# A four-layer graph kernel: layer norm's factors by blocks, and the first d ahead of the packings

## The chip, the cores and the metric

The kernel runs on one core of a Trainium2 chip. The time is the device time of one execution in microseconds (us); for the kernel before, the median of three runs is 541.25 us (540.78 to 541.6). A profiled execution is slower than these and is told apart from them.

A core has five queues of instructions that matter here, each worked off in its own order: PE (matrix products; PEld loads their weights), DVE (vector operations), ACT (activation functions and copies), POOL (here gathers by index, and a few fills) and SP (plain DMA transfers). Between them stand waits: an instruction starts when what it reads has been written and what it overwrites has been read.

## The reference

There are 2,708 nodes with 128 features, `x`, and an adjacency matrix `adj` of 2,708 by 2,708, of which about 0.3% are not zero; the entries of a row are all equal. Four layers follow one another, each of them with a layer norm and a ReLU ahead and added to its input:

```python
h = jnp.maximum(_layernorm(x, axis=-1), 0.0)
x = x + _L0_gnn_ref(h, adj, ...)      # hyperbolic maps around  adj @ log_map_zero(h)
h = jnp.maximum(_layernorm(x, axis=-1), 0.0)
x = x + _L1_gnn_ref(h, adj, ...)
# inside L1, for each pair i, j with an edge:
s = node_feats @ msg_w[:, :D].T
d = node_feats @ msg_w[:, D:].T
messages = gelu(s[:, None, :] + d[None, :, :] + msg_b)
aggregated = jnp.einsum('ijd,ij->id', messages, adj)
```

Layers 2 and 3 are products with `adj` again. The change lies in layer 0 and in what prepares layer 1.

## The kernel before

**Tiles.** The nodes lie in 22 tiles of 128 (the last has 20 nodes). Tiles go in six blocks, `groups[0]` to `groups[5]`: five of four tiles and one of two. Blocks 0 to 2 are the first half (12 tiles), blocks 3 to 5 are called `late`. `adj` transposed is read once, block by block, and kept as a mask of zeros and ones in one byte each (`read_block`, lines 1014 to 1055).

**Layer 0, product.** For each block the PE multiplies the mask with the node features, which are split into three bf16 parts: `add_product` (line 1359) does 22 tiles by 3 parts, 66 matmuls, into one accumulator `acc`; `end_product` (line 1375) squares and copies it and sums the squares (`nsq`). `neighbours` (line 1408) then makes the hyperbolic factors, `update` (line 1449) adds the result to `x` and takes the layer norm's statistics (`bn_stats`), and `normal_form` (line 944) makes scale and bias of the norm (`rstd`, `nb`) from them: 15 small DVE instructions, each needing the last.

**Edges.** In the same stretch the edges are found. `words_in` (line 1073) packs a block's mask into words: 22 matmuls `pk` on PE, a copy `wt` on ACT, transposes `wp` on PE, and a copy back. The last block is narrower than its tiles, so that POOL fills the rest of `wt` with zeros first (line 1082). `find_words`, `find_columns` and `lay_out` on DVE make lists of neighbours from the words; `val` is gathered by POOL for each tile (line 1160), and `po` is a small matmul in `lay_out` (line 1256).

**Preparing layer 1.** `make_d` (line 1473) takes a block: ACT makes h from x with `rstd` and `nb` (line 961), PE transposes it (`hTpm`, line 971), it is copied (`hT`, line 972), PE multiplies it with the message weights (`d`, line 983), ACT copies the result (line 1480) and SP writes it to tables in HBM (line 1483): to `d_hbm`, which holds all nodes, and to `d_early`, two small tables with the first two and the first three blocks. The two first places of each tile's list of neighbours, the early places, are filled from `d_early` while layer 0 still runs (`gather_early`, line 1577, on POOL, one gather for one tile and place); the other places are gathered from `d_hbm` in layer 1 (line 1793), after its last write.

**What sets the order.** The function's text gives an order, but a planner lays out each engine's instructions by its own costs, and `queue_behind(i)` says that what follows is not placed ahead of instruction i. The built program's order on each engine is fixed.

**Layer 1 to 3.** Layer 1 goes tile by tile: POOL gathers, DVE adds, ACT makes the gelu, PE sums (lines 1802 to 1880), and products for layer 2 are put between. Layers 2 and 3 follow.

Of the kernel before, what the change touches and what calls it, by code (L numbers as in the profile page):

```python
# [51 lines left out]
BLOCK = 4  # L52
SLOTS = 24
HEAD = 6
EARLY = 2
# [501 lines left out]
def sparse_stack(  # L557
# [21 lines left out]
    nc = tc.nc  # L579
    N = x_in.shape[0]  # L580
    T = -(-N // P)
    NP = T * P
    full = N // P
# [27 lines left out]
    hT = state.tile([P, NP], F32, name="hT")  # L611
# [98 lines left out]
    early_c = state.tile([P, T, EARLY], U32, name="early_c")  # L710
# [55 lines left out]
    def queue_behind(ins):  # L766
        return ExitStack() if ins is None else tc.issue_after(ins.ins)
# [56 lines left out]
    with ExitStack() as st:  # L824
# [52 lines left out]
        def node(name):  # L877
            if name not in names:
                names[name] = wide.tile([P, T], F32, name=f"n_{name}")
            return names[name]  # L880
# [4 lines left out]
        def norm(sq, sl, name):  # L885

            a, r, n, q = (node(c + name)[:, sl] for c in "arnq")
            nc.vector.tensor_scalar_max(a, sq, NORM_EPS * NORM_EPS)
            rsqrt(a, r, q)
            nc.vector.tensor_mul(n, a, r)  # L890
            return a, r, n
# [52 lines left out]
        def normal_form(sl):  # L944

            t, a, r, nb, q = (node(name)[:, sl] for name in ("tn", "an", "rstd", "nb", "qn"))
            nc.vector.tensor_sub(t, bst[:, sl, 1], bst[:, sl, 4])
            nc.vector.tensor_mul(t, t, t)
            nc.vector.tensor_add(a, bst[:, sl, 2], bst[:, sl, 5])
            nc.vector.scalar_tensor_tensor(a, t, float(D // 4), a, op0=ALU.mult, op1=ALU.add)  # L950
            nc.vector.tensor_scalar(a, a, 1.0 / D, LN_EPS, op0=ALU.mult, op1=ALU.add)
            rsqrt(a, r, q)
            nc.vector.tensor_add(t, bst[:, sl, 1], bst[:, sl, 4])
            return nc.vector.scalar_tensor_tensor(nb, t, -0.5, r, op0=ALU.mult, op1=ALU.mult)
# [21 lines left out]
        def tiles_times(sl, aT, w, name, mirrored=False):  # L976

            n = sl.stop - sl.start
            ps = ps_one.tile([P, BANK], F32, tag="one", name=name)
            wide_by = w.shape[-1]  # L980
            for k in range(n):
                t = sl.stop - 1 - k if mirrored else sl.start + k
                latest["times"] = nc.tensor.matmul(  # L983
                    ps[:, k * wide_by : (k + 1) * wide_by],
                    aT[:, t * P : (t + 1) * P],
                    w,
                    start=True,
                    stop=True,
                )
            return ps[:, : n * wide_by].rearrange("p (n d) -> p n d", d=wide_by)  # L990
# [62 lines left out]
        def read_block(b):  # L1053
            for g in pieces:
                read_piece(b, g)
# [17 lines left out]
        def words_in(b, after=None):  # L1073

            t0, t1 = blocks[b]
            n = t1 - t0
            sl = cols(t0, t1)
            w = sl.stop - sl.start
            pk = pack(b, after)
            wt = words_p.tile([P, BANK], F32, tag="wt", name=f"wt{b}")  # L1080
            if w < n * P:
                nc.gpsimd.memset(wt[:, w : n * P], 0.0)
            nc.scalar.copy(wt[:, :w], pk[:, :w])
            ps = ps_one.tile([P, BANK], F32, tag="one", name=f"wp{b}")
            for k in range(n):
                nc.tensor.transpose(ps[:, k * P : (k + 1) * P], wt[:, k * P : (k + 1) * P], ident)
            key = wt.bitcast(I32)
            nc.scalar.copy(key[:, : n * P], ps[:, : n * P])
            return key
# [78 lines left out]
        def each(c, n):  # L1168
            return c.unsqueeze(1).to_broadcast([P, n, EARLY])
# [189 lines left out]
        def add_product(b, acc, ts, after=None):  # L1359

            sl = cols(*blocks[b])
            w = sl.stop - sl.start
            for t in ts:
                for k in range(3):
                    with queue_behind(after):
                        last = nc.tensor.matmul(  # L1366
                            acc[:, :w],
                            parts[:, t, k, :],
                            mask[:, t, sl],
                            start=(t == 0 and k == 0),  # L1370
                            stop=(t == T - 1 and k == 2),
                        )
            return last
# [72 lines left out]
            nc.vector.tensor_add(dot[:, sl], dot[:, sl], node("dot0")[:, sl])  # L1446
            return last

        def update(bs):

            sl = slice(blocks[bs[0]][0], blocks[bs[-1]][1])
            f, ca, cb = node("f")[:, sl], node("ca"), node("cb")
            _, r, n = norm(node("sq")[:, sl], sl, "u")
            log_factor(node("nsq")[:, sl], f, sl)
            moebius(f, r, n, node("dot")[:, sl], y2_layer, ca[:, sl], cb[:, sl], sl)
            for b in bs:
                g = groups[b]
                n = g.stop - g.start
                for t in range(g.start, g.stop):
                    nc.vector.scalar_tensor_tensor(  # L1460
                        x[:, t, :], own[:, t, :], ca[:, t : t + 1], x[:, t, :], op0=ALU.mult,
                        op1=ALU.add,
                    )
                for t in range(g.start, g.stop):
                    nc.vector.scalar_tensor_tensor(
                        x[:, t, :], layer_b, cb[:, t : t + 1], x[:, t, :], op0=ALU.mult,
                        op1=ALU.add,
                    )
                for t in range(g.start, g.stop):
                    nc.vector.bn_stats(bst[:, t, :], x[:, t, :])  # L1470
            return normal_form(sl)

        def make_d(bs, copy, after=None, relu_after=None):

            for b in bs:
                g = groups[b]
                normal_tiles(g, f"m{b}", copy, after, relu_after)
                ps = tiles_times(g, hT, msg_w[:, 1, :], f"d{b}", mirrored=True)
                d = v[:, g, :]
                nc.scalar.copy(d, ps)  # L1480
                for table, end in ((d_early[0], reach[0]), (d_early[1], reach[1]), (d_hbm, T)):
                    if g.stop <= end:
                        nc.sync.dma_start(
                            out=table[(end - g.stop) * P : (end - g.start) * P, :].rearrange(
                                "(t p) d -> p t d", p=P
                            ),
                            in_=d,
                        )
# [88 lines left out]
        def gather_early(ts, ks):  # L1577
            for t in ts:
                for k in ks:
                    nc.gpsimd.indirect_dma_start(  # L1580
                        out=early_d[t // EACH][:, t % EACH, k, :],
                        out_offset=None,
                        in_=d_early[k],
                        in_offset=bass.IndirectOffsetOnAxis(ap=early_c[:, t, k : k + 1], axis=0),
                    )
# [17 lines left out]
        sums = sums_of([2])  # L1603
        product(2, sums)
        times = times_layer([2])
        formed = update([0, 1])
        read_block(4)
        acc = begin_product(3)
        last = add_product(3, acc, range(2 * BLOCK))
        read_block(5)  # L1610
        words[4] = words_in(4, last)
        last = latest["pack"]
        make_d([0], nc.scalar.copy, last)
        last = add_product(3, acc, range(2 * BLOCK, 3 * BLOCK), last)
        words[5] = words_in(5, last)
        last = latest["pack"]
        lay_out(halves[0])
        with queue_behind(scaled):
# [10 lines left out]
                is_place, place_k, 0.0, is_place, op0=ALU.is_ge, op1=ALU.mult  # L1629
            )  # L1630
        done = neighbours([2], sums, formed, times)
        make_d([1], nc.scalar.copy, last, latest["th"])
        find_words(3, words[3])
        find_columns(groups[3])
        for k in range(-(-T // EACH)):
# [7 lines left out]
        end_product(3, acc, sums)  # L1643
        acc = begin_product(4)
        last = add_product(4, acc, range(2 * BLOCK))
        formed = update([2])
        find_words(4, words[4], done)
        find_words(5, words[5], done)
        make_d([2], nc.scalar.copy, last)
        add_product(4, acc, range(2 * BLOCK, T), last)  # L1650
        end_product(4, acc, sums)
        product(5, sums)
        find_columns(slice(groups[3].stop, T))
        gather_early(range(first_half), [1])
        lay_out(halves[1])
        for b in (0, 1):
            mark_edges(b, formed)
        last = neighbours(late, sums)

        with queue_behind(last):  # L1660
            nc.vector.tensor_add(early_c[:, halves[1], :], late_c, each(none_c, T - first_half))
        gather_early(range(first_half, full), range(EARLY))
        formed = update(late)
        make_d(late, nc.vector.tensor_copy)
        for b in (2, *late):
            mark_edges(b, formed)
# [457 lines left out]
```

## Time and profile before

| | |
|---|---|
| median of three runs | 541.25 us |
| profiled execution | 634.93 us |
| its span, from first to last instruction | 633.2 us |
| mean granted clock of PE in it | 0.841 of full |
| busy in it: PE, DVE, ACT, POOL | 439.5, 425.7, 243.1, 234.4 us |
| layer 0 and preparing layer 1 (to the first gather from `d_hbm`) | 0 to 238.5 us |
| gathers of layer 1 | 238.5 to 477.8 us |
| rest | 477.8 to 633.2 us |

A group of the profile is read so: line and engine, operation, tile written and tiles read (without buffer numbers), how often; then the busy time in us and the mean duration in ns; then the idle time of the engine just ahead of it, and what ended most of it. In a timeline, the first number is the start in us from the span's beginning, the second the length, and the bracket the idle time ahead and what ended it. "issue" means that nothing is shown that the engine waited for, "remote" and "another core or an unknown queue" that what released it is not known.

### The profile page before, as it was taken

The page shows a single profiled execution, that of the slowest core. Times are in us where ns is not written, and L with a number is a line of the kernel's source. Part 1 is how long each engine was busy: PE and PEld are TensorE (multiplying, and loading weights), DVE is VectorE, ACT ScalarE, POOL GpSimd, SP SyncE. Part 2 cuts the span into 40 slices and gives each one's busy share as a digit, 9 for nine tenths or more (in the row PEclk, how much of TensorE's full clock was granted, in tenths as well). Part 3 has the DMA queues.
Part 4 walks back from the last instruction along what each step waited for, and adds up shares of the span by engine and source line. Part 5 has one row for each costly group of instructions (what it writes and reads, how often), then busy time and mean ns, then how long its engine had stood idle before and what let it go on. Part 6 is the DMA issues. An engine that isn't in the chain of part 4 may idle for free.

```text
span 633.2 us, 8305 instructions
## 1 busy us (share of the span) xinstructions
PE 439.5 (69%) x2504; PEld 278.4 (44%) x2504; DVE 425.7 (67%) x1805; ACT 243.1 (38%) x576; POOL 234.4 (37%) x269
## 2 busy tenths in 40 slices
PE   2955999997185061335756658737849898989995
PEld 1641445453144051234625436525636544545553
DVE  7959869988314975533758557646736669998752
ACT  3787668872012133112534423423435544510000
POOL 8600132015551747755754655655741000000000
PEclk9986999999595556656778977977979999989999
DMA  8884698613020121211315345344310024079311
GB/s 278 261 300 146 227 332 284 188 53 85 15 68 16 46 71 41 51 41 44 89 43 191 104 130 162 95 125 152 103 38 10 1 89 175 2 285 391 128 37 57
DMA packets 40420, 78.41 MB, mean 124 GB/s; under 512 B 5818, under 2 KB 19702, under 8 KB 38810
## 3 DMA queue, kind: packets, MB, share of 16 engines
q1 hardware_dynamic: 31326, 63.67, 29.2%
q0 software_dynamic: 7296, 13.40, 8.4%
q10 hardware_dynamic: 1744, 0.72, 0.4%
q8 instruction: 22, 0.36, 0.2%
q14 instruction: 32, 0.26, 0.1%
HBM read 73.63 MB, written 4.14 MB: 123 GB/s over the span
## 4 chain that ended last, share of the span: by engine, by line
DVE 34%; PE 29%; another core or an unknown queue 11%; issue 11%; ACT 8%; DMA 5%; POOL 2%; ACTq 0%; DVEq 0%; POOLq 0%
PE three L1732 8%; PE two L1732 4%; PE msg L1855 4%; DMA a<-in_adj_t_dram 2%; PE msg L1857 2%; DMA layer_w<-in_L_gnn_layer_dram 2%; DVE eq L1748 2%; PE own L801 2%; PE d L983 1%; POOL g L1793 1%; PE u L1516 1%; ACT mask L1034 1%; PE acc L1366 1%; PE neigh L1771 1%
## 5 line engine op out<-in xcount | busy, mean ns | idle before, releaser
L1732 PEld LDWEIGHTS <-parts 128*128 128x128 bf16 x792 | 76.1, 101 | 85.6 <-issue 8.0
L1793 POOL DMA_INDIRECT g<-d_hbm,head_c x84 | 83.2, 991 | 75.6 <-issue 39.0
L1732 PE MATMUL two<-mask,parts 128*128 128x512 fp8e4 (+1 forms) x396 | 85.0, 370 | 5.8 <-ACT parts L1717 5.5
L1366 PE MATMUL acc<-mask,parts 128*128 128x512 fp8e4 (+1 forms) x396 | 84.0, 366 | 6.2 <-issue 5.8
L1732 PE MATMUL three<-mask,parts 128*128 128x512 fp8e4 (+1 forms) x396 | 80.5, 359 | 0.6 <-ACT parts L1717 0.5
L1793 POOL DMA_INDIRECT gt<-d_hbm,tail_c x65 | 62.6, 963 | 27.5 <-issue 18.3
L1366 PEld LDWEIGHTS <-parts 128*128 128x128 bf16 x396 | 38.0, 102 | 53.6 <-issue 9.3
L1580 POOL DMA_INDIRECT early<-d_early,early_c x42 | 42.2, 1005 | 49.7 <-issue 21.4
L1855 PE MATMUL msg<-ident,early 128*128 128x128 f32 x84 | 19.1, 364 | 56.7 <-DVE gt L1844 27.2
L1160 POOL DMA_INDIRECT val<-in_adj_dram,ai x22 | 21.0, 957 | 78.1 <-DVE left L1148 64.2
L1034 ACT ACTIVATE mask<-a 128x2048 fp8e4<-128x2048 uint32 (+3 forms) x27 | 38.2, 1431 | 9.2 <-DMA a<-in_adj_t_dram 8.7
L1855 PEld LDWEIGHTS msg<-ident,early 128*128 128x128 f32 x84 | 14.9, 248 | 60.4 <-issue 43.3
L1748 DVE TENSOR_SCALAR_CACHE_REDUCE eq<-row,val 128x2708 fp8e4<-128x2708 f32 (+1 forms) x13 | 39.4, 3030 | 1.1 <-DMA row<-in_adj_dram 1.0
L1064 PE MATMUL pk<-mask,shifts 128*128 128x512 fp8e4 (+1 forms) x132 | 30.9, 374 | 12.5 <-ACT mask L1034 12.5
L1844 DVE TENSOR_TENSOR gt<-gt,msg 128x384 f32<-128x384 f32 (+1 forms) x22 | 12.0, 544 | 29.9 <-remote 28.4
L1855 PE MATMUL msg<-ident,g 128*128 128x128 f32 x168 | 31.5, 348 | 0.0
L1808 PE MATMUL msg<-parts,r_all 128*128 128x128 bf16 x195 | 15.0, 224 | 22.5 <-issue 18.5
L1855 PEld LDWEIGHTS msg<-ident,g 128*128 128x128 f32 x168 | 29.9, 262 | 0.5
L1831 DVE TENSOR_TENSOR rt<-col_i,tail_r 128x384 f32<-128x384 f32 (+1 forms) x22 | 12.0, 552 | 26.8 <-remote 21.7
L1748 DVE TENSOR_SCALAR_CACHE_REDUCE eq<-hT,val 128x1354 fp8e4<-128x1354 f32 x18 | 29.2, 1620 | 0.1
L1850 ACT ACTIVATE gt<-gt 128x384 f32<-128x384 f32 (+1 forms) x22 | 11.4, 517 | 37.9 <-DVE gt L1844 23.5
L1869 ACT COPY aggs<-msg 128x128 f32<-128x128 f32 x22 | 5.7, 261 | 51.4 <-remote 31.3
(408 smaller groups left out, 919.8 us busy)
## 6 DMA issues: line engine op xcount, KB each, us to landing
a<-in_adj_t_dram SPq DMA_DIRECT2D x25, 1024.0 KB
row<-in_adj_dram SPq DMA_DIRECT2D x12, 1354.0 KB
hT<-in_adj_dram SPq DMA_DIRECT2D x18, 677.0 KB
a<-in_adj_t_dram SPq DMA_DIRECT2D x5, 296.0 KB
g<-d_hbm,head_c POOLq DMA_INDIRECT x84
a<-in_adj_t_dram SPq DMA_DIRECT2D x5, 256.0 KB
d_early<-v SPq DMA_DIRECT2D x5, 256.0 KB
d_hbm<-v SPq DMA_DIRECT2D x5, 256.0 KB
```

The lines of the kernel that those rows point to most:

```text
L801: nc.tensor.matmul(ps[:, k, :, :], hT[:, (t + k) * P : (t + k + 1) * P], pair_w[:, 0::2, :], start=True, stop=True,)
L1034: nc.scalar.activation(mask[:, g : g + n, sl], bits[:, :n, :w], AF.Sign, saturate=False)
L1064: latest["pack"] = nc.tensor.matmul(pk[:, :w], shifts[:, t, :], mask[:, t, sl], start=(t == 0), stop=(t == T - 1),)
L1160: nc.gpsimd.indirect_dma_start(out=val[:, t : t + 1], out_offset=None, in_=flat, in_offset=bass.IndirectOffsetOnAxis(ap=ai[:, t : t + 1], ...
L1366: last = nc.tensor.matmul(acc[:, :w], parts[:, t, k, :], mask[:, t, sl], start=(t == 0 and k == 0), stop=(t == T - 1 and k == 2),)
L1580: nc.gpsimd.indirect_dma_start(out=early_d[t // EACH][:, t % EACH, k, :], out_offset=None, in_=d_early[k], in_offset=bass.IndirectOffsetOn ...
L1732: last = nc.tensor.matmul(accs[b][:, : sl.stop - sl.start], parts[:, t, k, :], mask[:, t, sl], start=(t == 0 and k == 0), stop=(t == T - 1 ...
L1748: last = nc.vector.tensor_scalar(eq[:n, : c1 - c0], a, val[:n, t : t + 1], None, op0=ALU.is_equal, op1=ALU.add, accum_out=same[:n, t, k : ...
L1793: nc.gpsimd.indirect_dma_start(out=g[:n, q, :], out_offset=None, in_=d_hbm, in_offset=bass.IndirectOffsetOnAxis(ap=table[:n, q : q + 1], a ...
L1808: latest["source"] = nc.tensor.matmul(ps[:, q * D : (q + 1) * D], r_all[:, t, q * P : (q + 1) * P], parts[:, t, k, :], start=(k == 0), sto ...
L1855: nc.tensor.matmul(sums, part, ident, start=(q == 0), stop=False)
L1857: done = nc.tensor.matmul(sums, gt[:, q, :], rt[:, q, :], start=(not own_places and q == 0), stop=(q == nq - 1),)
```

## The change

Four things are changed in layer 0.

- `update` takes a list `ends` of blocks after which `normal_form` is made, each time for the tiles since the last. The first call, for blocks 0 and 1, makes it after each of the two; the last, for blocks 3 to 5, after block 4 and after block 5. The call for block 2 makes one, as before.
- `make_d` of blocks 0 and 1 goes ahead of the packings of blocks 4 and 5 on PE, with tiles of product 3 between. It stood behind the packing of block 4 and of block 5.
- `make_d` of block 2 has four tiles of product 4 between its transposes and its product with the weights (`between`).
- The early places of the late tiles are gathered in another order: the late tiles' first place goes ahead of the first half's second place. For it, `early_c`, the index, is made in two pieces, one for each place, where it was one; `lay_out` of the second half stands ahead of these gathers.

```diff
-        def update(bs):
+        def update(bs, ends):
 
             sl = slice(blocks[bs[0]][0], blocks[bs[-1]][1])
             f, ca, cb = node("f")[:, sl], node("ca"), node("cb")
+            form = None
...
                 for t in range(g.start, g.stop):
                     nc.vector.bn_stats(bst[:, t, :], x[:, t, :])
-            return normal_form(sl)
-
-        def make_d(bs, copy, after=None, relu_after=None):
+                if b in ends:
+                    form = slice(form.stop if b > ends[0] else sl.start, g.stop)
+                    last = normal_form(form)
+            return last
+
+        def make_d(bs, copy, after=None, relu_after=None, between=None):
 
             for b in bs:
                 g = groups[b]
                 normal_tiles(g, f"m{b}", copy, after, relu_after)
-                ps = tiles_times(g, hT, msg_w[:, 1, :], f"d{b}", mirrored=True)
+                with queue_behind(between() if between else None):
+                    ps = tiles_times(g, hT, msg_w[:, 1, :], f"d{b}", mirrored=True)
...
-        formed = update([0, 1])
+        formed = update([0, 1], [0, 1])
         read_block(4)
         acc = begin_product(3)
-        last = add_product(3, acc, range(2 * BLOCK))
+        last = add_product(3, acc, range(6))
+        make_d([0], nc.scalar.copy, last)
+        last = add_product(3, acc, range(6, 9), last)
         read_block(5)
+        make_d([1], nc.scalar.copy, last)
+        last = add_product(3, acc, range(9, 3 * BLOCK), last)
         words[4] = words_in(4, last)
-        last = latest["pack"]
-        make_d([0], nc.scalar.copy, last)
-        last = add_product(3, acc, range(2 * BLOCK, 3 * BLOCK), last)
-        words[5] = words_in(5, last)
+        words[5] = words_in(5, latest["pack"])
         last = latest["pack"]
         lay_out(halves[0])
...
         done = neighbours([2], sums, formed, times)
-        make_d([1], nc.scalar.copy, last, latest["th"])
         find_words(3, words[3])
...
-        formed = update([2])
+        formed = update([2], [2])
         find_words(4, words[4], done)
         find_words(5, words[5], done)
-        make_d([2], nc.scalar.copy, last)
-        add_product(4, acc, range(2 * BLOCK, T), last)
+        make_d(
+            [2],
+            nc.scalar.copy,
+            last,
+            between=lambda: add_product(4, acc, range(2 * BLOCK, 3 * BLOCK), last),
+        )
+        add_product(4, acc, range(3 * BLOCK, T), last)
         end_product(4, acc, sums)
         product(5, sums)
         find_columns(slice(groups[3].stop, T))
+        lay_out(halves[1])
+        early_tail = early_c[:, halves[1], :]
+        nc.vector.tensor_add(
+            early_tail[:, :, 0:1], late_c[:, :, 0:1], each(none_c, T - first_half)[:, :, 0:1]
+        )
+        gather_early(range(first_half, full), [0])
         gather_early(range(first_half), [1])
-        lay_out(halves[1])
         for b in (0, 1):
             mark_edges(b, formed)
         last = neighbours(late, sums)
 
         with queue_behind(last):
-            nc.vector.tensor_add(early_c[:, halves[1], :], late_c, each(none_c, T - first_half))
-        gather_early(range(first_half, full), range(EARLY))
-        formed = update(late)
+            nc.vector.tensor_add(
+                early_tail[:, :, 1:], late_c[:, :, 1:], each(none_c, T - first_half)[:, :, 1:]
+            )
+        gather_early(range(first_half, full), [1])
+        formed = update(late, [late[-2], late[-1]])
         make_d(late, nc.vector.tensor_copy)
```

## The prediction

> **What bounds the kernel now.** I read the page first, then the answer by cores (one core, mean granted clock 0.841), the chain of waits, and the timeline of layer 0 from 95 us on, engine by engine.
>
> ```profile
> span 633.2 us, 8305 instructions
> DVE 34%; PE 29%; another core or an unknown queue 11%; issue 11%; ACT 8%; DMA 5%; POOL 2%; ACTq 0%; DVEq 0%; POOLq 0%
> L1793 POOL DMA_INDIRECT g<-d_hbm,head_c x84 | 83.2, 991 | 75.6 <-issue 39.0
> L1793 POOL DMA_INDIRECT gt<-d_hbm,tail_c x65 | 62.6, 963 | 27.5 <-issue 18.3
> ```
>
> The profiled execution took 634.93 us (span 633.2, 1.7 around it), the median of the runs is 541.25, 93.7 less. The second line names where I look for those: 11% of the span (71.6 us) ends on an unknown queue, waits that no semaphore of the program explains. I treat them as the profiled execution's own; everything below is a shift in us, carried over to the median.
>
> The message passing of layer 1 gathers 84 + 65 = 149 times on POOL, one each 1.25 us where POOL is not held (0.94 plus 0.30 of issue): 186 us. In the profile it takes 238.5 to 477.8, 239 us. What follows takes 155 us. In a run of 541 us, 155 behind it leaves its end near 384 and its start near 198 to 209: there POOL goes nearly back to back, so what moves the first g gather moves the end by as much.
>
> Next the first gather. In the timeline (start, length, engine, line, what; in brackets the idle time before and who ended it) of POOL:
>
> ```profile
> 130.40 0.21 POOL L1082 MEMSET wt<- 128x108 f32 x1
> 146.30 0.95 POOL L1580 DMA_INDIRECT early<-d_early,early_c  x1 [15.69 <-DMA d_early<-v]
> ...
> 229.05 0.94 POOL L1580 DMA_INDIRECT early<-d_early,early_c  x1 [0.30 <-issue]
> 238.54 1.17 POOL L1793 DMA_INDIRECT g<-d_hbm,head_c  x1 [8.55 <-DMA d_hbm<-v]
> ```
>
> So g waits for the last d_hbm write, not for the early gathers. Behind that write stand make_d and update of the late chunks, and these begin when PE has finished products 4 and 5. PE's timeline:
>
> ```profile
> 127.99 4.91 PE L1064 MATMUL pk<-mask,shifts 128*128 128x512 fp8e4 x22
> ...
> 139.58 0.44 PE L1086 MATMUL wp<-ident,wt 128*128 128x128 f32 x2
> ...
> 148.23 1.04 PE L1389 MATMUL nsq<-ones_col,hT 128*128 128x1 f32 x8
> ...
> 172.46 2.07 PE L983 MATMUL d<-pair_w,hT 128*128 128x128 f32 x8 [17.55 <-ACT hT L972]
> ```
>
> and of ACT and DVE what PE waited for, and what waited for PE; last a line of the chain of waits:
>
> ```profile
> 171.82 0.59 ACT L972 COPY hT<-hTpm 128x512 f32<-128x512 f32 x1 [20.62 <-remote]
> ...
> 198.99 0.17 DVE L1413 TENSOR_TENSOR n_nsq<-nsq,val 128x10 f32<-128x10 f32 x1 [1.08 <-PE nsq L1389]
> ```
>
> ```profile
> 235.20 2.49 DMA d_hbm<-v
> ```
>
> PE stands still nowhere from 124 to 154 us; then ACT waits 20.62 us for nothing named. Without that, PE's d goes at 154.9 and ends at 156.05 (1.15, as the one at 141.21); 38 matmuls of 512 columns by 0.216 (22 packings from 127.99 to 132.74) make 164.25, 66 of 148 columns by 0.067 (30 in 2.09) and 1.05 of nsq 169.75, and 1.9 from po to the last nsq 171.65. So n_nsq, which opens the late chunks, is at 171.7 undisturbed. From there to the landing the profile has 237.69 - 198.99 = 38.7, less 2.0 that DVE's hT copy is held at 229.72: 36.7. **d_hbm lands at 208.4.** POOL undisturbed: 12 early gathers from 146.3 to 161.5, six val to 169.0, 12 and 18 more early ones to 206.5 (208.7 if some stretch as they do in the profile, where the 18 took 24.5). The two paths lie 2 us apart, d_hbm's behind.
>
> [...]2.49 for d_hbm and 3.3 from the end of d's copy (142.97) to the first early gather. [...]2.07 for the eight d passes after 17.55 us of standing, 1.14 in the busy stretch.
>
> **The change, part by part.** I compared the order in which both kernels, built, stand on each engine.
>
> *Form by blocks, first update.* update([0, 1]) ends in two normal_forms instead of one: 15 DVE instructions more (0.08 each where others lie between, 0.20 where each waits for the last). The first stand between the 12 instructions of block 1: 121.4 + 12 x 0.26 + 15 x 0.08 puts block 0's n_nb at 125.6 (127.5 now), block 1's at 128.6, since its chain takes 3.1 us as now, only 1.2 later. So neighbours([2]) starts 1.2 later. DVE is not what the end hangs on here: 13 us of its work lie between 149.4 and PE's 171.7.
>
> *First d ahead of the packings.* PE: 12 matmuls of acc 3, transposes of block 0, d, block 1, d, then packings 4 and 5. The same matmuls, moved ahead of 6.6 us of packings. Transposes now follow ACT's relus directly: PE is there at 126.7, the third relu at 127.1, and the copy of hT comes behind one mask on ACT: 0.3 + 0.4 of standing, **0.7** (0 to 1.5). SP's six writes of the two d (two d_early and one d_hbm each, 0.36 to 0.56 of issue) move ahead too; SP's last read of block 5 was issued at 125.7, so they pass nothing. Block 1's d ends at 133.7, ACT copies it by 134.4 (four squares of neighbours first), and POOL can gather at 134.4 + 3.3 = **137.7** instead of 146.3.
>
> *What is queued behind that wait.* In the new order POOL has six early gathers in front of the memset of wt (L1082), which now stands ahead of them at 130.40. The memset fills the tail of block 5's words; PE's second wp transpose waits for POOL. Six gathers by 1.25 from 137.7: the memset ends at 145.4. PE would be at the transposes at: d 133.7, three matmuls 0.65, packing 4 4.75, packing 5 and wp 4 2.2, two matmuls 0.4: 141.6. **PE stands 3.8 us** (2.5 to 5: both times hang on the same d, so their difference is firmer than each). Queued behind it: po, all of acc 3's rest, acc 4 and 5. DVE waits for po as well, and layer-norm of block 2 with it: n_off at 146.0, the rest of update([2]) and its form (1.7 + 0.6 + 3.75 with find_words between) end at 152.6; ACT has a relu of block 2 ahead of acc 3's square, so nsq follows at 153.7 where PE is at 152.95: **0.7** more (0 to 1.5). [...]
>
> *find_words 4 and 5* move behind update([2]): DVE reaches find_columns at 157, 8 us later; its 13 us end at 171, ahead of PE's 176.9, so nothing. But ai is ready at 160 (151.65 now), and POOL's val gathers wait there from 153.
>
> *make_d([2]) with four more tiles of product between* (12 matmuls instead of 4): d_early's second table 1.7 us later, at 166; POOL wants it at 179. Nothing.
>
> *Early places.* The 42 gathers stay; 9 go ahead, on a 10-wide addition more (0.17). POOL: 12 to 153, val 160.3 to 167.8, 9 to 179, 21 to 205.3. Now 206.5: 1.2 gained on the path that does not set the start.
>
> *Form by blocks, late update.* Block 4's form no longer waits for block 5's six instructions, but shares DVE with them: n_nb at 220.9 instead of 221.54; ACT's relus 0.6 earlier. Then marks stand in front of DVE's hT copy: 223.7 for 223.96. The rest is a chain of PE, DVE and ACT as before. **0.3 gained** (0 to 1.6, the whole of block 5's instructions).
>
> Sum: 0.7 + 3.8 + 0.7 - 0.3 = **+4.9**: n_nsq of the late chunks at 176.9, d_hbm at 213.3 for 208.4, POOL free at 205.3. 541.25 + 4.9 = 546.1; in terms of the profiled execution 634.93 + 4.9 = 639.8, if its own waits stayed, which they need not.
>
> **Rivals.** *The standing is covered* (POOL comes to the memset before PE comes to wp, or PE has enough spare time after): for it, that all these times are rebuilt, not read; against it, that the gathers cannot start sooner than d's landing, and d is only 8 us of PE work ahead of wp. Then +0.7 - 0.3: 541.6. *Faster:* not d_hbm but POOL's last early gather opens the messages undisturbed. Place: POOL after 184; price: 1.2 by the count, up to 3.4 if the 18 stretch to 208.7 as in the profile, say 2.2: 539.0. It decides only if d_hbm lands today before 200.4 (205.3 less the 4.9), 8 us sooner than I rebuilt; against it speaks the 8.55 that POOL waits in the profile, for it that 93.7 us of that execution are its own and I placed them by inference. *Dearer:* the half clock, a longer standing and late ai together: +8, 549.3.
>
> **Numbers.** Forecast 0.60 (own range 543.5 to 548.5), covered 0.15, faster 0.13, dearer 0.12. Range 540.9 to 549.0: it takes in forecast, covered and the near half of dearer, and leaves out most of faster. 0.2% is 1.1 us, about what the three runs' spread (0.8) lets one tell. Faster 0.13; same 0.11, most of the covered case; slower 0.76.
>
> **What the profile will show.** Right: POOL's memset behind six early gathers, PE's second wp transpose idle for 2.5 to 5 us and ended by that memset; the first early gather 8 to 9 us sooner against PE's packings; DVE's n_off waiting for po; g again ended by d_hbm. Wrong: wp without idle time; or g following early gathers directly, with POOL never idle before it.

## The result, and the profile after

The kernel before took 541.75 us in this comparison (median of 13 runs, 538.34 to 543.89), the changed kernel 547.07 us (13 runs, 542.66 to 549.18). The ratio is 1.0095, with a 95% interval of 1.0068 to 1.0121: 5.3 us slower, where 4.9 was forecast. The profile of before that the prediction read held some 94 us of waits that no run had (634.93 us for 541.25). A second profile of the same kernel (run e1 below, span 538.1 us) has none, so that a profiled execution is not slower as such; "before" in this part means the second one. Ratios leave out slow runs, those over 1.5% above the fastest of the same kernel: in e7 these are two of 17 (543.49 and 544.41 us).

From the page of the changed kernel: the span, the chain by engine, and the two groups of gathers.

```profile
span 545.1 us, 8338 instructions
DVE 35%; PE 28%; DMA 11%; ACT 10%; issue 9%; POOL 5%; ACTq 0%; DVEq 0%; SPq 0%; POOLq 0%
L1810 POOL DMA_INDIRECT g<-d_hbm,head_c x84 | 83.4, 993 | 32.3 <-issue 20.7 <-DMA d_hbm<-v 7.0 <-ACT jx L1720 0.6
L1810 POOL DMA_INDIRECT gt<-d_hbm,tail_c x65 | 64.2, 988 | 19.8 <-issue 16.2 <-ACT parts L1736 0.6 <-ACT u L1892 0.6
```

No share of the chain ends on an unknown queue here. POOL, in the timeline of the changed kernel (start, length, engine, line, what, idle time before and who ended it):

```profile
137.49 0.94 POOL L1585 DMA_INDIRECT early<-d_early,early_c  x1 [7.14 <-DMA d_early<-v]
...
143.78 0.95 POOL L1585 DMA_INDIRECT early<-d_early,early_c  x1 [0.30 <-issue]
144.73 0.21 POOL L1082 MEMSET wt<- 128x108 f32 x1
...
205.34 1.16 POOL L1585 DMA_INDIRECT early<-d_early,early_c  x1 [0.31 <-issue]
213.51 0.95 POOL L1810 DMA_INDIRECT g<-d_hbm,head_c  x1 [7.01 <-DMA d_hbm<-v]
```

The fill stands behind six early gathers, and the first g waits 7.01 us for the last write of d_hbm. PE of the same kernel:

```profile
128.78 1.16 PE L983 MATMUL d<-pair_w,hT 128*128 128x128 f32 x8 [1.20 <-ACT hT L972]
...
141.20 0.33 PE L1086 MATMUL wp<-ident,wt 128*128 128x128 f32 x1
144.99 0.48 PE L1086 MATMUL wp<-ident,wt 128*128 128x128 f32 x1 [3.46 <-POOL wt L1082]
145.33 8.79 PE L1366 MATMUL acc<-mask,parts 128*128 128x512 fp8e4 x33
```

The second transpose stands 3.46 us for the fill, as forecast, and the 33 matmuls behind it take 8.79 us. The trace shows the clock that they had. By windows of time (from and to, length, PE's busy time, its instructions, its granted clock as a share of full, the share of DMA and GB/s):

```profile
141.00:145.00 4.00, 0.54 (x4) 1.00 0.18 49
145.00:148.00 3.00, 3.00 (x9) 0.50 0.19 49
148.00:149.00 1.00, 1.00 (x6) 0.79 0.26 66
149.00:154.00 5.00, 5.00 (x26) 1.00 0.19 52
```

From 145 to 148 us the clock is at half; a mean of 0.79 in the microsecond behind is another 0.42 us of half clock (0.21 by 0.5), 3.4 us in all. The late d's of this kernel have a granted clock of 0.50 too (198 to 206 and 206 to 210 us) and take 2.07, 2.08 and 1.19 us; block 0's d, above, takes 1.16 at a granted 1.00 (128.5 to 130 us). By these times a d is said below to run at half or at full clock. And DVE:

```profile
145.54 0.17 DVE L1257 COPY n_off<-po 128x12 f32<-128x12 f32 x1 [5.38 <-PE po L1256]
...
175.81 0.17 DVE L1413 TENSOR_TENSOR n_nsq<-nsq,val 128x10 f32<-128x10 f32 x1 [0.34 <-PE nsq L1389]
```

The start of a profile differs by up to 2.5 us between executions (block 2's `ne` product starts at 120.18 to 122.70 us, with variants of both kernels near both ends). So below, times are counted from the start of that product, which stands ahead of everything that was changed. "Copy" is the start of ACT's last copy of d (line 1480 before, 1485 in the changed kernel), "POOL free" the end of the last early gather; the last column is span less start of g.

| kernel (one profile of each) | n_nsq of the late blocks | copy | POOL free | first g | from g to the end |
|---|---|---|---|---|---|
| before (e1) | 47.97 | 82.04 | 86.05 | 86.35 | 331.6 |
| changed | 53.40 | 87.15 | 84.09 | 91.10 | 331.6 |
| e2 fill first | 48.91 | 82.40 | 80.60 | 86.21 | 331.1 |
| e3 fill last | 60.29 | 92.14 | 82.73 | 96.16 | 333.2 |
| e4 d ahead alone | 53.54 | 87.60 | 84.84 | 91.52 | 330.9 |
| e5 d back | 48.94 | 81.05 | 86.28 | 86.59 | 331.7 |
| e6 fill first, early order back | 48.67 | 82.52 | 78.80 | 86.76 | 330.9 |
| e7 fill first, unread matmuls | 48.57 | 79.36 | 79.19 | 83.53 | 330.8 |
| e8 before, unread matmuls | 47.95 | 79.68 | 86.44 | 86.75 | 332.4 |
| e9 stand filled | 51.65 | 83.51 | 82.10 | 87.59 | 332.1 |
| e10 e7 and marks behind | 48.79 | 78.99 | 78.71 | 83.66 | 335.4 |
| e11 e7 again | 48.17 | 81.09 | 78.29 | 84.46 | 331.2 |
| e12 unread matmuls throughout | 48.76 | 79.47 | 79.36 | 82.84 | 331.8 |

From g to the end, the changed kernel and the kernel before take the same 331.6 us: all 4.75 us by which the two profiles differ from that product on lie ahead of the first g.

### The profile page after: what moved, and what is told of

The parts are those of the page before. It is cut to its first block, busy times and chain, and to the rows that moved or that the text cites. A ratio compares the mean times of both kernels' runs of the same rounds, so it can differ in the third digit from the quotient of the medians.

```text
span 545.1 us, 8338 instructions
## 1 busy us (share of the span) xinstructions
PE 418.4 (77%) x2504; PEld 263.8 (48%) x2504; DVE 426.4 (78%) x1836; ACT 242.9 (45%) x576; POOL 236.4 (43%) x269
## 4 chain that ended last, share of the span: by engine, by line
DVE 35%; PE 28%; DMA 11%; ACT 10%; issue 9%; POOL 5%; ACTq 0%; DVEq 0%; SPq 0%; POOLq 0%
PE three L1749 9%; DMA a<-in_adj_t_dram 6%; PE acc L1366 5%; PE msg L1872 3%; POOL g L1810 3%; DVE eq L1765 3%; ACT mask L1034 2%; DMA g<-d_hbm,head_c 2%; PE two L1749 2%; DMA layer_w<-in_L_gnn_layer_dram 2%; ACT h L1730 1%; PE msg L1874 1%; PE d L983 1%; DVE gt L1861 1%; DVE g L1858 1%
## 5 line engine op out<-in xcount | busy, mean ns | idle before, releaser
L1749 PEld LDWEIGHTS <-parts 128*128 128x128 bf16 x792 | 74.4, 99 | 80.1 <-ACT parts L1734 4.9
L1749 PE MATMUL two<-mask,parts 128*128 128x512 fp8e4 (+1 forms) x396 | 81.8, 359 | 3.8 <-ACT parts L1734 3.5
L1366 PEld LDWEIGHTS <-parts 128*128 128x128 bf16 x396 | 37.1, 100 | 46.3 <-ACT parts L786 7.5
L1872 PE MATMUL msg<-ident,early 128*128 128x128 f32 x84 | 16.7, 329 | 30.8 <-DVE gt L1861 22.6
L1872 PEld LDWEIGHTS msg<-ident,early 128*128 128x128 f32 x84 | 13.0, 218 | 34.5 <-DVE gt L1861 12.8
L961 ACT ACTIVATE h<-x,n_nb,n_rstd 128x128 f32<-128x128 f32 x44 | 18.3, 485 | 20.7 <-DVE n_qn L778 11.5
L1872 PE MATMUL msg<-ident,g 128*128 128x128 f32 x168 | 27.2, 313 | 0.0
L1872 PEld LDWEIGHTS msg<-ident,g 128*128 128x128 f32 x168 | 25.5, 228 | 0.2
L1825 PEld LDWEIGHTS <-r_all 128*128 128x128 fp8e4 x195 | 13.1, 104 | 19.9 <-issue 14.0
L1858 DVE TENSOR_TENSOR g<-g,v 128x512 f32<-128x512 f32 x21 | 14.4, 688 | 10.3 <-DMA g<-d_hbm,head_c 9.7
L971 PE MATMUL hTpm<-ident,h 128*128 128x128 f32 x22 | 5.7, 353 | 21.0 <-ACT h L961 21.0
```

What stands on the lines that cost most here:

```text
L961: nc.scalar.activation(h[:, t, :], x[:, t, :], AF.Relu, bias=node("nb")[:, t : t + 1], scale=node("rstd")[:, t : t + 1],)
L1366: last = nc.tensor.matmul(acc[:, :w], parts[:, t, k, :], mask[:, t, sl], start=(t == 0 and k == 0), stop=(t == T - 1 and k == 2),)
L1749: last = nc.tensor.matmul(accs[b][:, : sl.stop - sl.start], parts[:, t, k, :], mask[:, t, sl], start=(t == 0 and k == 0), stop=(t == T - 1 ...
L1825: latest["source"] = nc.tensor.matmul(ps[:, q * D : (q + 1) * D], r_all[:, t, q * P : (q + 1) * P], parts[:, t, k, :], start=(k == 0), sto ...
L1858: nc.vector.tensor_add(a, a, v[:, t, :].unsqueeze(1).to_broadcast([P, a.shape[1], D]))
L1872: nc.tensor.matmul(sums, part, ident, start=(q == 0), stop=False)
```

## Experiments

**e1: the kernel before again.**

> The kernel before, unchanged, for a second profile of it: the first held some 92 us of waits of its own, and the prediction rebuilt the stretch around them. Theory (d's last write to d_hbm opens layer 1's messages): in a profile without those waits n_nsq of the late blocks stands at 171.7 us, POOL is done with the early gathers at 206.5 to 208.7, and the first g gather waits 1 to 2 us for d_hbm, at about 208.9. Rival (POOL's own early gathers open the messages): g follows the last early gather by 0.3 us, with d_hbm landed before it. Time in both cases about 541.7 us.

Measured: 539.91 us in its one run. POOL and DVE in its timeline:

```profile
205.27 0.96 POOL L1580 DMA_INDIRECT early<-d_early,early_c  x1 [0.30 <-issue]
206.53 1.08 POOL L1793 DMA_INDIRECT g<-d_hbm,head_c  x1 [0.30 <-issue]
```

```profile
168.15 0.17 DVE L1413 TENSOR_TENSOR n_nsq<-nsq,val 128x10 f32<-128x10 f32 x1 [0.95 <-DMA val<-in_adj_dram,ai]
```

The rival is right: g follows the last early gather by 0.30 us. But not by much. The chain of waits shows POOL's sequencer (POOLq) done with its waits of line 1793, that for d_hbm among them, ahead of g. First e1, then the changed kernel, where g waits for d_hbm alone:

```profile
205.73 0.04 POOLq L1793
205.78 0.76 issue
```

```profile
212.78 0.04 POOLq L1810
212.82 0.70 issue
```

In both, g follows the second of these lines directly. With the 0.70 us of the changed kernel in place of 0.76, d_hbm would have let g go in e1 at 206.47, 0.06 us sooner than it went. Two paths end within 0.1 us of each other. The DVE line shows a wait that the prediction did not have: n_nsq waits for POOL's val gathers, which stand behind twelve early gathers here, and not for PE.

**e2: the fill ahead of the early gathers.** One instruction of POOL is moved in the changed kernel.

```diff
-                nc.gpsimd.memset(wt[:, w : n * P], 0.0)
+                latest["fill"] = nc.gpsimd.memset(wt[:, w : n * P], 0.0)
...
-        gather_early(range(first_half), [0])
+        with queue_behind(latest["fill"]): gather_early(range(first_half), [0])
```

> The changed kernel with one instruction moved: POOL's fill of the last words (memset of wt) stands ahead of the early gathers, as in the kernel before; every other engine's order is untouched. Theory (the standing of PE behind that fill is the loss): PE's second wp transpose no longer stands (3.46 us in the changed kernel's profile), the 33 matmuls behind it go at 0.216 us each for 0.266 (8.79 us become 7.1), n_nsq of the late blocks is at 170.7 for 175.8 us, and the time falls by 3.5 to 5.1 us from the changed kernel's 547.07, to 542.0 to 543.6. Rival (the loss lies in the earlier d, the forms by blocks or the gathers' order): within 0.7 us of the changed kernel, 546.4 to 547.8.

Measured: 540.87 us (22 runs), ratio to before 0.9978 (0.9954 to 1.0002). PE in its timeline:

```profile
140.41 0.44 PE L1086 MATMUL wp<-ident,wt 128*128 128x128 f32 x2
140.68 0.17 PE L1256 MATMUL po<-tailn,tri 128*128 128x12 bf16 x1
140.71 7.28 PE L1366 MATMUL acc<-mask,parts 128*128 128x512 fp8e4 x33
148.72 1.05 PE L1389 MATMUL nsq<-ones_col,hT 128*128 128x1 f32 x8 [0.73 <-ACT hT L1384]
```

The stand is gone, the 33 matmuls take 7.28 us for 8.79 (0.22 us each for 0.27), n_nsq comes 4.5 us sooner and g 4.9 us. The whole loss is won back by one fill, and the theory holds. The median falls by 6.2 us, more than the expected 3.5 to 5.1 and more than g moves; what the rest is, the profile doesn't show. 0.73 us of the stand return as a wait for ACT, whose relu of block 2 is ahead of product 3's square. POOL is now free 5.6 us before g.

**e3: the fill behind all twelve.** For block 5, `words_in` stops behind ACT's copy, and its rest (the fill, queued behind the last of these gathers, then the transposes wp and the copy back) is called after them.

```diff
-        words[5] = words_in(5, latest["pack"])
+        words[5] = words_in(5, latest["pack"], hold=True)
...
         gather_early(range(first_half), [0])
+        words[5] = words[5](latest["early"])
```

> The changed kernel with the fill of wt moved the other way: behind all twelve early gathers instead of six. PE now has po and five matmuls of product 3 ahead of the second transpose instead of behind it. Theory (each further gather ahead of the fill holds PE for 1.25 us): the fill ends 7.5 us later, at 152.5 us; PE comes to it 1.3 later, so it stands 9.7 instead of 3.46 us, and the time is 6.2 us more than the changed kernel's, about 553.3 (552 to 555). Rival (the stand is made up for later, or POOL sets the start of the messages): 547.1, within 1 us of the changed kernel.

Measured: 551.66 us (6 runs), ratio 1.0170 (1.0126 to 1.0214). Its second transpose on PE:

```profile
151.04 0.48 PE L1096 MATMUL wp<-ident,wt 128*128 128x128 f32 x1 [10.40 <-POOL wt L1086]
```

It stands 10.40 us for the 9.7 expected, and n_nsq comes 6.9 us behind the changed kernel's. The copy is only 5.0 us later and the time 4.6 us longer instead of 6.2: two of the three late d's happened to run at full clock here (1.16 us for eight passes and 0.68 for four; 2.08 and 1.19 in the changed kernel). The dose acts on the stand and on n_nsq as the theory says; the time is below the expected 552 to 555, and the clock of the late d's accounts for that in this profile (see e7 to e12).

**e4: d ahead of the packings, alone.** The kernel before, with the two old calls of `make_d` for blocks 0 and 1 taken out and these put in.

```diff
         acc = begin_product(3)
-        last = add_product(3, acc, range(2 * BLOCK))
+        last = add_product(3, acc, range(6))
+        make_d([0], nc.scalar.copy, last)
+        last = add_product(3, acc, range(6, 9), last)
         read_block(5)
+        make_d([1], nc.scalar.copy, last)
+        last = add_product(3, acc, range(9, 3 * BLOCK), last)
         words[4] = words_in(4, last)
...
```

> The kernel before with one of the four edits alone: d of blocks 0 and 1 ahead of the packings of blocks 4 and 5. The layer norm's forms, block 2's d and the order of the early places stay as before. POOL's fill stands behind six early gathers here too. Theory (this edit carries the whole loss, through the fill): PE stands 3 to 4.5 us at the second wp transpose, and the time is that of the changed kernel or 0.3 more, 546.5 to 548.5. Rival (a good part of the loss is due to another of the edits): below 545.5; none of it due to this one: 541.7.

Measured: 549.58 us (6 runs), ratio 1.0153 (1.0112 to 1.0193), above the expected 546.5 to 548.5. The second transpose stands 4.13 us for the fill, n_nsq lies within 0.14 us of the changed kernel's, and g comes 0.4 us later. So this edit is enough for the whole loss. Its profiled run was the fastest of the six (545.37 us); why the others are some 4 us longer isn't seen in it, and whether the other three edits give back 1 to 3 us of it stays open.

**e5: d back, the other three edits kept.** The text of e4's diff is turned round in the changed kernel.

> The changed kernel with d of blocks 0 and 1 back behind the packings, as in the kernel before; the forms by blocks, block 2's d with four tiles between, and the new order of the early places are kept. The fill then stands ahead of the early gathers again. Theory (the earlier d, through the fill, carries the whole loss; the other three edits are worth little): PE stands nowhere at wp, the late chain from n_nsq to d's last copy is 0.3 us shorter, and POOL's gathers, as many as before, end at about the same time; the ratio to the kernel before is 0.998 to 1.001, 541.5 to 543 us. Rival (one of the other three edits costs by itself): 1.004 or more, 545 us or more.

Measured: 542.37 us (14 runs), ratio 0.9988 (0.9964 to 1.0012). As expected: forms by blocks, block 2's d with tiles between and the new order of early places, taken together, cost nothing and bring nothing that the runs tell. Its POOL shows why an earlier d_hbm wouldn't help there: the copy comes 1 us sooner than in e1 (two of its late d's ran at full clock, 1.16 and 0.68 us), but g follows the last early gather by 0.30 us, at 86.59.

**e6: the old order of early places, in e2's kernel.**

```diff
-        gather_early(range(first_half, full), [0])
         gather_early(range(first_half), [1])
...
-        gather_early(range(first_half, full), [1])
+        gather_early(range(first_half, full), range(EARLY))
```

> The changed kernel with the fill ahead of the gathers, and the early places in the order of the kernel before (the late tiles' first place behind the first half's second). Theory (the order moves POOL's waits alone, and POOL is done 5.6 us ahead of the last d_hbm write there): the last early gather ends up to 1.5 us later, g still waits for d_hbm, and the time is that of the same kernel with the new order, 541 us (540 to 542). Rival (the order matters for the start of the messages): g follows the last early gather by 0.3 us, and the time is 1 us or more longer.

Measured: 540.91 us (20 runs), ratio 0.9968 (0.9949 to 0.9987). POOL is free at 78.80 with the old order, at 80.60 in e2 and at 79.36, 79.19 and 78.29 in e12, e7 and e11 with the new one. Of an effect of the order, on the time or on POOL, nothing is seen.

**e7: unread matmuls ahead of the late blocks.** In e2's kernel PE stands still for 20.74 us and then runs the late transposes and d's at half clock (the d's take 2.07, 2.08 and 1.19 us), on the path to d_hbm. This fills the end of the gap.

```diff
+        warm = ps_one.tile([P, BANK], F32, tag="one", name="warm")
+        with queue_behind(latest["times"]):
+            for t, many in ((blocks[lead][0], 12), (blocks[-1][0], 10)):
+                nc.tensor.transpose(warm[:, :P], x[:, t, :], ident)
+                for k in range(many):
+                    nc.tensor.matmul(
+                        warm, parts[:, k, 0, :], mask[:, k, :BANK], start=True, stop=True
+                    )
         make_d(late, nc.vector.tensor_copy)
```

> The changed kernel with the fill ahead of the gathers, and 24 matmuls on PE whose result nobody reads, from block 3's last update of x on, so that PE does not stand still for 21 us ahead of the late blocks' transposes. Theory (the late d's run at half clock after that idle time: 2.07 us for eight passes which take 1.13 in the busy stretch): transposes and d's of the late blocks take 0.43, 0.92, 0.43, 0.93, 0.2 and 0.5 us less; part of it is taken by DVE's marks, so d_hbm lands 2 to 3.3 us sooner, POOL is free by then, and the time is 537.5 to 539.5 us, ratio to before 0.989 to 0.995. Rival (POOL or DVE sets the time there, or the clock does not rise): 540.5 to 541.5, ratio 0.997.

Measured: 539.76 us (17 runs), ratio 0.9941 (0.9910 to 0.9972). All three late d's run at full clock (1.16, 1.16 and 0.68 us; 2.08, 2.08 and 1.19 in e1. On the page the granted clock is 9 tenths in the slice from 187.9 to 201.3 us; in e1's it is 5 from 188.3 to 201.8), the copy comes 3.0 us and g 2.7 us sooner than in e2. The ratio is in the expected range; e2's interval and this one overlap.

**e8: the same matmuls in the kernel before.**

> The kernel before with the same 24 unread matmuls on PE ahead of the late transposes. Theory (in the kernel before POOL's last early gather opens the messages: in its second profile g follows it by 0.3 us, with d_hbm due only 0.4 us earlier): the late d's run at full clock, d_hbm lands 2 to 3.3 us sooner, g does not move, and the ratio is 0.998 to 1.002. Rival (d_hbm's last write sets the start of the messages in the kernel before): the ratio is 0.992 to 0.996, 2 to 3.3 us less.

Measured: 542.20 us (14 runs), ratio 1.0006 (0.9974 to 1.0037). The copy comes 2.4 us sooner than in e1, g 0.4 us later. POOL:

```profile
208.20 0.94 POOL L1580 DMA_INDIRECT early<-d_early,early_c  x1 [0.30 <-issue]
209.45 0.94 POOL L1801 DMA_INDIRECT g<-d_hbm,head_c  x1 [0.30 <-ACT parts L786]
```

A shorter way to d_hbm is worth nothing in the kernel before, in the profile and in the time, where POOL is busy until g. In e7's profile, where the earlier d has made POOL free sooner, it is worth 2.7 us; the time of that is less sure (e11). So e1's reading holds: in the kernel before POOL's gathers bound g too.

**e9: the stand filled.** In the changed kernel, 14 unread matmuls stand between the two transposes, so that PE is busy while it waits.

```diff
...
+                if w < n * P and k == 0:
+                    idle = ps_one.tile([P, BANK], F32, tag="one", name="idle")
+                    with queue_behind(turn):
+                        for m in range(14):
+                            nc.tensor.matmul(
+                                idle, parts[:, m, 0, :], mask[:, m, :BANK], start=True, stop=True
+                            )
```

> The changed kernel, its fill where it is (behind six early gathers), with 14 unread matmuls of 512 columns on PE between the first and the second wp transpose, 3.0 us at 0.216 each, so that PE works while it waits for the fill. The planner moves DVE's n_off and some find_words with it. Theory (the stand costs twice: 3.46 us by itself, and 1.65 because the 33 matmuls behind it take 8.79 us for 7.15): the stand stays, the 33 matmuls take 7.1 to 7.3 us, n_nsq and g come 1.3 to 1.7 us sooner relative to the ne product of block 2, and the time is 545.4 (544.9 to 546). Rival (the slower matmuls have another cause, transfers or the weights' loads beside them): they stay at 0.26 us, and the time at 547.

Measured: 543.54 us (22 runs), ratio 1.0032 (1.0014 to 1.0051). PE:

```profile
141.33 3.19 PE L1093 MATMUL idle<-mask,parts 128*128 128x512 fp8e4 x14
144.96 0.33 PE L1086 MATMUL wp<-ident,wt 128*128 128x128 f32 x1 [0.44 <-POOL wt L1082]
145.15 7.07 PE L1375 MATMUL acc<-mask,parts 128*128 128x512 fp8e4 x32
```

The fill still comes when it came, but the matmuls behind it take 0.22 us each for 0.27, as they do in e2 without the stand, and n_nsq comes 1.75 us sooner: the second price of the stand is the clock, the 0.50 granted behind it in the changed kernel. The time falls by more than that (3.5 us against the changed kernel's median; 544.9 to 546 was expected); in this profile two of the late d's also ran at full clock (1.16 and 0.68 us), which takes another 1.9 us from the way to the copy. Whether that was so in all 22 runs can't be seen.

**e10, e11: marks behind the copies of hT, and e7 again beside it.** In e10, e7's kernel, the marks (DVE's `mark_edges`, two instructions for each tile) are queued behind the last copy of hT.

```diff
         for b in (2, *late):
-            mark_edges(b, formed)
+            mark_edges(b, latest["hT"])
```

> The changed kernel with the fill ahead of the gathers and the 24 unread matmuls, and DVE's marks (before, r_all) of blocks 2 to 5 behind the late blocks' three copies of hT. In the run without this edit DVE is in the marks until 196.13 us where PE's transposes end at 195.4. Theory (d_hbm's last write still opens the messages, POOL being free 4.3 us earlier): PE's first late d starts 0.7 us sooner, g comes 0.7 to 0.9 us sooner, and the time is 0.7 to 0.9 us less than that of the kernel without this edit. Rival (the marks are due for the first tail gathers, or POOL's order of g and gt, which the planner changes, matters): the same time or up to 2 us more.

> The kernel with the fill ahead of the gathers and the 24 unread matmuls once more, beside the one with the marks moved. Theory: as in its first run, ratio to before 0.991 to 0.997, about 3 us less than the kernel before. Rival: the first ratio was chance, and this one is above 0.997.

Measured: e10 542.66 us (22 runs), ratio 1.0014 (0.9994 to 1.0035); e11 540.72 us (14 runs), ratio 0.9992 (0.9967 to 1.0017). Both went the rival's way. In e10 the copy comes 0.4 us sooner than in e7, but g starts no sooner (83.66 for 83.53), and the first g itself takes five times as long:

```profile
205.76 4.86 POOL L1818 DMA_INDIRECT g<-d_hbm,head_c  x1 [4.95 <-DMA d_hbm<-v]
```

DVE runs its postponed marks back to back until about 210.6, where that gather ends. In e11 the clock did not hold (the second late d takes 2.07 us for the first one's 1.16); PE in its timeline:

```profile
195.68 1.16 PE L983 MATMUL d<-pair_w,hT 128*128 128x128 f32 x8 [1.43 <-DVE hT L972]
196.67 1.02 PE L971 MATMUL hTpm<-ident,h 128*128 128x128 f32 x4
198.47 2.07 PE L983 MATMUL d<-pair_w,hT 128*128 128x128 f32 x8 [0.78 <-DVE hT L972]
```

The first d is fast, the second falls back, and g comes 0.9 us later than in e7. So e7's gain is not sure in each execution. The two were timed on different chips, each beside the kernel before; whether that plays a part is open.

**e12: unread matmuls in the holes too.** To those ahead (now 12 and 12) come 12 more, for which `unread(n, i)` puts n of them behind instruction i: one between each two transposes of block 3, and 4, 3 and 2 behind the three groups of transposes, where PE waits for DVE's copies.

```diff
                 for k in range(n):
-                    nc.tensor.transpose(ps[:, k * P : (k + 1) * P], h[:, sl.start + k, :], ident)
+                    turn = nc.tensor.transpose(
+                        ps[:, k * P : (k + 1) * P], h[:, sl.start + k, :], ident
+                    )
+                    if k + 1 < n:
+                        unread(1 if sl.start == blocks[lead][0] else 0, turn)
+                unread({blocks[lead][0]: 4, blocks[-1][0]: 2}.get(sl.start, 3), turn)
```

> The changed kernel with the fill ahead of the gathers, and unread matmuls not only ahead of the late blocks' transposes (24 and two transposes) but also between and behind them (12 more), where PE waits for ACT's relus and DVE's copies of hT. In the two runs with the unread matmuls ahead alone, all late d's ran at full clock once (1.16, 1.16, 0.68 us), and once the second and third fell back to half clock (2.07, 1.19). Theory ([...]with fewer holes it stays up): all late d's take 1.13 to 1.16 and 0.68 us, the last copy of d ends 79.3 to 80 us behind the start of block 2's ne product (82.4 in the kernel before), g comes 2 to 3 us sooner than in the kernel before, and the ratio is 0.992 to 0.996. Rival (the gain of the first of these runs was chance, or g is held by something else): d's at half clock again, or a ratio above 0.997.

Measured: 537.14 us (6 runs, 535.14 to 538.85), ratio 0.9900 (0.9854 to 0.9946). PE:

```profile
195.40 1.16 PE L998 MATMUL d<-pair_w,hT 128*128 128x128 f32 x8 [0.50 <-DVE hT L987]
196.39 0.60 PE L981 MATMUL hTpm<-ident,h 128*128 128x128 f32 x4
196.83 0.81 PE L962 MATMUL warm<-mask,parts 128*128 128x512 fp8e4 x3
197.78 1.16 PE L998 MATMUL d<-pair_w,hT 128*128 128x128 f32 x8
```

All late d's are at full clock, and g comes 3.5 us sooner than in the kernel before, where 2 to 3 were expected. The ratio allows 2.9 to 7.9 us. This is the fastest kernel here, but it has six runs and one profile and was not tried again; the intervals of e6 and e7 leave out 1 too, and e7 did not repeat it. These matmuls were not put into the kernel before; e8 makes it likely that they would bring nothing there, since POOL is not free sooner.

## Why the prediction was right, step by step

The forecast (546.1 us, the stand as cause) held: e2, e3, e4 and e9 show it from four sides. Its sum came out at 4.9 for 4.75 between the two profiles, but partly by luck, because errors cancelled.

- **What bounds the kernel.** "d_hbm lands at 208.4 ... d_hbm's behind" failed in its second half. The rebuilt n_nsq was good (171.7 with `ne` 3.04 us later than in e1 is 168.7; e1 has 168.15). POOL was not: 206.5 is 203.5 in e1's count, and it was free at 206.23. The step counted each early gather at 1.25 us; in e1 all 42 take 1.02 us on average beside 0.30, single ones 2.08, and the value that stood in brackets, 208.7, was the nearer one. So the rival "faster" had the mechanism of the kernel before right (POOL opens the messages), but with d_hbm only 0.06 us ahead it could not decide: that slack alone came off the loss.
- **First d ahead.** 0.7 us of standing forecast, 1.20 measured (0.18 to 0.96 in the runs with this order of PE). The first early gather came 8.0 us sooner in this count (15.08 us behind `ne` for 23.08); 8.6 were forecast.
- **The stand at the fill.** 3.8 forecast, 3.46 measured; 4.13 in e4.
- **Half clock.** Not in the forecast's sum, only in its dearer rival: 8.79 us for 33 matmuls less e2's 7.28 for the same 33 is 1.51. This is the term that was mis-sized.
- **nsq behind ACT.** 0.7 forecast, none measured: with slow matmuls PE came to nsq no earlier than ACT's square. Where they are fast (e2) the 0.73 us are there. The two terms exclude each other in part, which the sum did not see.
- **val.** Not in the prediction: from PE's last nsq to n_nsq it takes 1.36 us in e1, 0.64 in the changed kernel, since n_nsq no longer waits for val. 0.72 us gained. The step on early places looked at POOL's end alone and not at who waits for val in between.
- **Late form by blocks.** 0.3 gained forecast; from n_nsq to the copy 33.75 us for 34.07, 0.32. All three late d's ran at half clock in both profiles (2.08, 2.08 and 1.19 us in e1; 2.07, 2.08 and 1.19 in the changed kernel).
- **From the copy to g.** Taken as unchanged; 3.95 us in the changed kernel, and 4.25 in e1 to the 206.47 at which d_hbm would have let g go. 0.30 us gained, with no edit there; the step takes 3.37 to 4.67 us in the runs whose g waits for d_hbm.
- **First form, find_words, block 2's d, early places.** Nothing, as forecast (e5); the 1.2 us that POOL was to gain by the order are not there (e6). That POOL is free 2 us sooner comes from the earlier d: 84.84 in e4, which has it alone, and 86.28 in e5, which lacks it alone.

The sum as measured: 1.20 + 3.46 + 1.51 is 6.17, for 6.15 at PE's last nsq (52.76 for 46.61); less 0.72 for val 5.43 at n_nsq; less 0.32 for the form 5.11 at the copy; less 0.30 from the copy on and the slack of 0.06 it is 4.75 at g, and the end follows g. From n_nsq on each term is a difference of the same two profiles, so that the sum must close; it is no test of its own.

## What to carry to other kernels

When gathers move ahead on a queue, look for what they move past: here one fill of 0.21 us, with PE waiting for it, cost 5 us, and putting it back in front of them won all of it. The stand on PE cost more than its length, since the matmuls behind it ran slower (1.51 us beside 3.46); reckon both. Where nothing useful can be moved into such a gap on the path, matmuls that nobody reads can fill it (e9, e12). Where two paths end together, shortening one showed nothing (e8), and both together did (e12; e7 in one of two comparisons), so measure the pair.

## What was not expected of the hardware

A stand of 3.46 us was enough for half clock (granted 0.50 from 145 to 148 us in the changed kernel), 1.51 us on the path. The spell at half clock lasted 3.4 us there. Behind longer stands the matmuls were slow too: 31 took 8.54 us in e4 behind 4.13, 0.28 us each, and 28 took 8.06 in e3 behind 10.40, 0.29 each, for 0.22 in e2. After the gaps of 20.74 to 22.36 us ahead of the late transposes the same instructions ran at either clock in different kernels and executions: the second late d took 2.08 us in e1, e2, e4, e6 and the changed kernel, and 1.16 in e3, e5 and e9, with no edit near it in these three. In e11, where unread matmuls fill part of the gap, it took 2.07, and in e7, with the same kernel, 1.16. What sets the moment at which the clock changes is not shown by these runs. In the one profile of e12 fewer holes went with a clock that stayed up (the late d's took 1.16, 1.16 and 0.71 us).

In e10 a gather that takes 0.94 us elsewhere took 4.86, until DVE's marks ended, at about 210.6 us. What held it is not shown: gathers beside the same marks in e1 took 0.94 to 2.08 us and were mostly not held, and what sets the difference was not tried.
